# Self-attention's output projection of six token tiles as 2 by 2 blocks, with the sequences in another order

## The chip, the cores and the metric

The kernel runs on one core of a Trainium2 chip. The metric is the device time of one execution in microseconds; three runs of the kernel before gave 1006.05 us as the median, from 1003.74 to 1006.45. A profile of one execution tells when each engine was busy and what it waited for. The engines are TensorE (PE; its weight loads are shown apart as PEld), VectorE (DVE), ScalarE (ACT), GpSimd (POOL) and SyncE (SP), which here issues DMAs. Each engine works through its own queue in order, and waits on semaphores that others raise.

## The reference

One decoder layer in fp32: x + self-attention(norm(x)), then cross-attention to a context, then a mixture of experts with a shared expert. The change touches the first part alone. There are 8 sequences of 112 tokens, width 512, 16 heads of 128:

```
k, q, v = W_K x, W_Q x, W_V x        # per head: 128 x 512
attn = softmax(causal mask of q k / sqrt(128))
z = attn v                           # per head: 112 x 128
out = W_O z_flat                     # W_O: 512 x 2048 (16 heads x 128)
x = x + out
```

## The kernel before

The 896 tokens are kept as 7 tiles of 128. Tile t holds the 112 tokens of sequence t + 1 and 16 tokens of sequence 0, so sequence 0 is spread over the ends of all tiles (`seq` and `like_seq` translate). The layer norm's output is kept transposed in `xn1`.

Self-attention goes through four groups `g` of four heads (`GH`), and in each group through these steps.

- *Queries and keys* (`pair_of_heads`, matmuls on line 274): qT and kT, channels by tokens, for two heads at a time. These products are already done as 2 by 2 blocks: seven products of sums in place of eight products, with the sums of the tokens (`xc`) made once, and the sums of the weights made on GpSimd for each pair (`t`, pool `w_sums`, tag `wc`, three buffers).
- *Values* (`values_left`, `values`, line 393): the same scheme, seven products of 128 x 256 for each of three pairs of tiles. `values` is a generator; every `next` emits one product. Some rows are moved with DMAs from SP: each sequence's values must start at partition 0, and the 16-row tails of sequence 0 are gathered into `vals[0]`.
- *Each sequence b*: `softmax` (scores s on TensorE, line 191; scale, mask and maximum on VectorE; exponentials on ACT), `normalise` (reciprocal on VectorE, product on GpSimd, line 216), `turn` (transposes on TensorE, line 222, copy on ACT), `weighted` (z on TensorE, line 230, copy into `zT` on VectorE, line 237).
- *Output projection* (`project_o`, line 432): for tile t, four matmuls of 128 x 512, one for each head, added up in PSUM with `wog`, this group's part of W_O; VectorE adds the result to `xs[t]` (line 439). In the last group the statistics of the second norm are taken straight after it (`ln_stats`, into `mv2`).

The order in which these are written out is that of the loop at the end of the group: five sequences (1, 2, 3, 0, 4) go through softmax beside the value products; then one sequence after the other is weighted, with the softmax of the one that comes four later and the turning of the next one before it. Sequence 0 is weighted with sequence 4, and tiles are projected from there on, the last three at the end. A scheduler then orders the instructions of each engine by these priorities, and each engine keeps that order. The matmuls' results go through eight PSUM buffers: four in pool `mm` (q products, values, projection) and four in `sc` (k products, scores, turned scores, z). The first group's `wcp` buffers, `part` buffers (`p1`, `p5`, `u2`, `u3`, two each) and `qT`, `kT`, `zT` (one buffer each) are shared by all steps and groups.

After the last group, cross-attention starts with the key projections of the first context (three chunks, line 517), and with the second norm: standard deviations of tiles 0 to 3 in one instruction, of tiles 4 to 6 in another.

Of the kernel before, what the change touches and what calls it, by code (L numbers as in the profile page):

```python
# [15 lines left out]
F32 = mybir.dt.float32  # L16
I32 = mybir.dt.int32
AF = mybir.ActivationFunctionType
ALU = mybir.AluOpType
AX = mybir.AxisListType  # L20

P = 128
B, S, D = 8, 112, 512
NT = B * S
TT = NT // P
SP = P - S
ND = D // P
HALF = NT // 2
H, DH = 16, 128
GH = 4  # L30
NG = H // GH
# [28 lines left out]
def seq(ap, b):  # L60

    if b:
        return ap[..., (b - 1) * P : (b - 1) * P + S]
    axes = " ".join("abcd"[: len(ap.shape) - 1])
    return ap.rearrange(f"{axes} (t i) -> {axes} t i", t=TT)[..., S:]


def like_seq(ap, b):

    if b:  # L70
        return ap
    axes = " ".join("abcd"[: len(ap.shape) - 1])
    return ap.rearrange(f"{axes} (t i) -> {axes} t i", t=TT)
# [3 lines left out]
def decoder_layer(  # L77
    ctx: ExitStack, tc: tile.TileContext, x, ctxT, wqk, wv_all, wo, wx, wgate, wsgu, wsd, wegu, wed_a, wed_b, consts, out
):
    nc = tc.nc  # L80
# [7 lines left out]
    mm = ctx.enter_context(tc.tile_pool(name="mm", bufs=4, space=PSUM))  # L88
# [14 lines left out]
    xs = []  # L103
# [13 lines left out]
    def psum(pool, name):  # L117
        return pool.tile([P, 512], F32, tag=pool.name, name=name)
# [18 lines left out]
    def ln_begin(name):  # L137
        return lnpool.tile([P, TT, 2], F32, tag="mv", name=f"mv_{name}")

    def ln_stats(mv, t):  # L140
        st = lnpool.tile([P, 6], F32, tag="st", name="st")
        nc.vector.bn_stats(st, xs[t])
        nc.vector.bn_aggr(mv[:, t, :], st)
# [32 lines left out]
    mv2 = ln_begin("2")  # L176
    with ExitStack() as sa:
        wvpool = sa.enter_context(tc.tile_pool(name="weights_vo", bufs=2))
        xcp = sa.enter_context(tc.tile_pool(name="x_sums", bufs=1))
        wcp = sa.enter_context(tc.tile_pool(name="w_sums", bufs=3))  # L180
        up = sa.enter_context(tc.tile_pool(name="part", bufs=2))
# [6 lines left out]
        def softmax(b, qT, kT, q0):  # L188
            ps = psum(sc, "s")
            for h in range(GH):  # L190
                nc.tensor.matmul(  # L191
                    like_seq(ps[:S, h * S : (h + 1) * S], b),
                    qT[:, h, (b - 1) * P : (b - 1) * P + S] if b else q0[:, h, :],
                    seq(kT[:, h, :], b),
                    start=True,
                    stop=True,
                )
            s = sp.tile([S, GH, S], F32, tag="s", name="s", bufs=5)
            nc.vector.scalar_tensor_tensor(
                out=s,  # L200
                in0=ps[:S, : GH * S].rearrange("q (h p) -> q h p", h=GH),
                scalar=float(DH) ** -0.5,
                in1=mask[:, None, :].to_broadcast([S, GH, S]),
                op0=ALU.mult,
                op1=ALU.add,
            )
            mx = sp.tile([S, GH], F32, tag="mx", name="mx")
            nc.vector.tensor_reduce(mx, s, AX.X, ALU.max, negate=True)  # L208
            sm = sp.tile([S, GH], F32, tag="sm", name="sm")
            for h in range(GH):  # L210
                nc.scalar.activation(s[:, h, :], s[:, h, :], AF.Exp, bias=mx[:, h : h + 1], accum_out=sm[:, h : h + 1])  # L211
            return s, sm

        def normalise(s, sm):
            nc.vector.reciprocal(sm, sm)  # L215
            nc.gpsimd.tensor_tensor(s, s, sm[:, :, None].to_broadcast([S, GH, S]), ALU.mult)  # L216
            return s

        def turn(s):
            pt = psum(sc, "pT")  # L220
            for h in range(GH):
                nc.tensor.transpose(pt[:S, h * S : (h + 1) * S], s[:, h, :], ident[:S, :S])
            sT = sp.tile([S, GH, S], F32, tag="sT", name="sT")
            nc.scalar.copy(sT, pt[:S, : GH * S].rearrange("p (h q) -> p h q", h=GH))
            return sT

        def weighted(b, sT, v, zT):
            pz = psum(sc, "z")
            for h in range(GH):
                nc.tensor.matmul(  # L230
                    pz[:, h * S : (h + 1) * S],
                    v[:S, h * DH : (h + 1) * DH],
                    sT[:, h, :],
                    start=True,
                    stop=True,
                )
            nc.vector.tensor_copy(
                seq(zT, b), like_seq(pz[:, : GH * S].rearrange("p (h q) -> p h q", h=GH), b)
            )
# [58 lines left out]
        for g in range(NG):  # L298
# [11 lines left out]
            wog = wvpool.tile([P, 4, 512], F32, tag="w", name=f"wo_{g}")  # L310
# [9 lines left out]
            qT = qkp.tile([P, GH, NT], F32, tag="qT", name="qT")  # L320
            kT = qkp.tile([P, GH, NT], F32, tag="kT", name="kT")
            zT = zp.tile([P, GH, NT], F32, tag="zT", name="zT")
            for h in range(0, GH, 2):
                for w, dst, pool in ((wq, qT, mm), (wk, kT, sc)):
                    if g == 0 and h == 0 and dst is qT:

                        for half in range(2):
                            cols = bass.ds(half * HALF, HALF)
                            for i in range(2):
                                ps = psum(mm, "qk")  # L330
                                for c in range(ND):
# [4 lines left out]
                                        start=(c == 0),  # L336
                                        stop=(c == ND - 1),
# [10 lines left out]
            soft, turned, vals = {}, {}, {}  # L348
# [20 lines left out]
            wide = D // 2  # L369
# [59 lines left out]
            def project_o(t):  # L429
                ps = psum(mm, "o")  # L430
                for h in range(GH):
                    nc.tensor.matmul(  # L432
                        ps,
                        zT[:, h, t * P : (t + 1) * P],
                        wog[:, h, :],
                        start=(h == 0),
                        stop=(h == GH - 1),
                    )
                nc.vector.tensor_tensor(xs[t], ps, xs[t], ALU.add)  # L439
                if g == NG - 1:  # L440
                    ln_stats(mv2, t)


            q0 = vp.tile([P, GH, S], F32, tag="q0", name="q0", bufs=1)
            nc.gpsimd.tensor_copy(like_seq(q0, 0), seq(qT, 0))
            values_left()
            products = values()
            for b in (1, 2, 3, 0, 4):
                weights = softmax(b, qT, kT, q0)
                next(products)  # L450
                next(products)
                soft[b] = normalise(*weights)
                next(products)
            turned[1] = turn(soft.pop(1))
            for b in range(1, B):
                for _ in zip(range(3), products):
                    pass
                if b + 4 < B:
                    weights = softmax(b + 4, qT, kT, q0)
                if b + 1 < B:  # L460
                    turned[b + 1] = turn(soft.pop(b + 1))
                if b == 3:
                    turned[0] = turn(soft.pop(0))
                weighted(b, turned.pop(b), vals.pop(b), zT)
                if b == 4:
                    weighted(0, turned.pop(0), vals.pop(0), zT)
                if b + 4 < B:
                    soft[b + 4] = normalise(*weights)
                if b > 3:
                    project_o(b - 4)  # L470
            for t in range(B - 4, TT - 2):
                project_o(t)
            project_o(TT - 2)
            project_o(TT - 1)

# [5 lines left out]
    with ExitStack() as xa:  # L483
# [13 lines left out]
        rawk, rawq, keys, queries, turned = {}, {}, {}, {}, {}  # L497
# [75 lines left out]
        def product(x, w):  # L573
            ps = psum(mm, "kv")
            for c in range(2):
                nc.tensor.matmul(ps[:MC, :], x[:, c, :], w[:, c, :], start=(c == 0), stop=(c == 1))  # L576
            return ps[:MC, :]
# [191 lines left out]
        for b in range(B):  # L769
# [29 lines left out]
            if b + 1 < B:  # L799
# [9 lines left out]
                if b + 2 == B:  # L809
                    sw = [load_shared(i) for i in range(2)]  # L810
                    ahead = wpool.tile([P, 4, 512], F32, tag="w", name="ahead")
# [10 lines left out]
    with ExitStack() as ff:  # L822
# [37 lines left out]
        part = rp.tile([P, NT], F32, name="part")  # L860
# [275 lines left out]
        for i in range(2):  # L1136
            g = gp.tile([P, HALF], F32, tag="g", name="g")
# [20 lines left out]
        h = {}  # L1158
# [109 lines left out]
```

## Time and profile before

| What | us |
|---|---|
| Median of three runs | 1006.05 |
| Profiled execution | 1006.36 |
| Its span, first to last instruction | 1004.6 |
| TensorE busy | 983.2 |
| VectorE, ACT, GpSimd busy | 388.0, 304.5, 284.2 |
| Start of the value products (line 364) of groups 0 to 3 | 61.9, 166.3, 270.8, 375.3 |
| Start of the key projections of cross-attention (line 517) | 437.7 |
| Granted clock of TensorE, mean | 0.999 |

A group of heads takes 104.5 us from one of these starts to the next. In a line of the groups, the names are out<-in, the shapes partitions x elements, then the number of instructions, the busy time in us, the mean of one in ns, and the idle time just before them. An fp32 matmul shows as two records on PE, each with its weight load on PEld; the records overlap, so that the pace is the distance from one start to the next and not the length of a record.

### The profile page before, as it was taken

Reading aid. Unit: us, or ns where it says so; the run is one execution under the profiler, and the core shown is the slowest. Engines: PE = TensorE matmul, PEld = TensorE weight load, DVE = VectorE, ACT = ScalarE, POOL = GpSimd, SP = SyncE. Lnnn points to the kernel's source line nnn. Section 1 sums busy time; section 2 is a strip of 40 time slices with the busy share of each in tenths; the row PEclk is TensorE's granted clock in tenths of the full one; section 3 lists DMA queues with packets and bytes.
Section 4 is the critical chain, followed back from the end, with each engine's and each line's share of the span. In section 5 each row is a group of like instructions: output and inputs, shape, how many; then the busy total and the mean of one; then the engine's idle time right before and its main releaser. Section 6 shows DMA issues by size and latency. Waiting matters only on the chain.

```text
span 1004.6 us, 15494 instructions
## 1 busy us (share of the span) xinstructions
PE 983.2 (98%) x5876; PEld 555.8 (55%) x5876; DVE 388.0 (39%) x765; ACT 304.5 (30%) x750; POOL 284.2 (28%) x310
## 2 busy tenths in 40 slices
PE   5999999999999999999999999999999999999998
PEld 3468555954596458645455555555565544444433
DVE  3335223622263235445432443434325243333324
ACT  2135011500152005314354455546543111111100
POOL 4245034603450243122533322331205600000032
PEclk9999999999999999999999999999999999999999
DMA  9522012201211112000000010000209748777765
GB/s 347 199 92 76 4 38 85 65 19 42 84 36 49 42 45 67 14 1 0 31 33 5 29 32 32 29 4 1 86 19 423 258 120 257 237 237 234 218 191 157
DMA packets 35320, 98.85 MB, mean 98 GB/s; under 512 B 4848, under 2 KB 10224, under 8 KB 31664
## 3 DMA queue, kind: packets, MB, share of 16 engines
q1 hardware_dynamic: 30192, 85.26, 25.6%
q0 software_dynamic: 2320, 7.63, 2.3%
q10 hardware_dynamic: 2736, 4.98, 1.7%
q8 instruction: 47, 0.77, 0.3%
q14 instruction: 25, 0.20, 0.1%
HBM read 78.85 MB, written 14.94 MB: 93 GB/s over the span
## 4 chain that ended last, share of the span: by engine, by line
PE 92%; issue 3%; DVE 2%; POOL 1%; DMA 1%; ACT 1%; SPq 0%; DVEq 0%; POOLq 0%; ACTq 0%
PE qk L274 16%; PE o L432 10%; PE kv L576 9%; PE v L393 7%; PE gu L838 5%; PE xs L671 5%; PE gate L1074 5%; PE y L1096 4%; PE up L1074 4%; PE pv L696 4%; PE ys L1122 3%; PE k L517 3%; PE xv L517 3%; PE z L230 3%; PE s L191 3%
## 5 line engine op out<-in xcount | busy, mean ns | idle before, releaser
L679 ACT ACTIVATE e<-xs 125x448 f32<-125x448 f32 x192 | 88.4, 544 | 72.4 <-PE xs L671 72.4
L432 PE MATMUL o<-wo,zT 128*128 128x512 f32 x224 | 99.3, 595 | 0.0
L274 PE MATMUL qk<-xc,wc 128*128 128x448 f32 x180 | 70.1, 539 | 0.0
L432 PEld LDWEIGHTS o<-wo,zT 128*128 128x128 f32 x224 | 41.3, 190 | 46.2 <-issue 45.9
L1107 POOL DMA_INDIRECT got<-routed,at x14 | 15.1, 1080 | 172.2 <-issue 171.2
L1074 PE MATMUL gate<-wex,xT 128*64 x144 | 55.3, 466 | 0.5 <-ACT xT L1039 0.5
L838 PE MATMUL gu<-xn,sw 128*128 128x448 f32 x144 | 55.5, 541 | 0.0
L211 ACT ACTIVATE s<-s,mx 112x112 f32<-112x112 f32 x128 | 48.1, 377 | 23.5 <-DVE mx L208 14.9
L1074 PE MATMUL up<-wex,xT 128*64 x144 | 54.3, 459 | 0.0
L274 PEld LDWEIGHTS qk<-xc,wc 128*128 128x128 f32 x180 | 34.2, 190 | 33.5 <-issue 32.3
L671 PE MATMUL xs<-qT,kT 32*125 32x224 f32 x768 | 50.4, 373 | 1.5 <-DVE qT L634 1.5
L671 PEld LDWEIGHTS xs<-qT,kT 32*125 32x125 f32 x768 | 33.2, 181 | 32.5 <-issue 27.7
L1024 DVE COPY xn<-wex 128x704 f32 x60 | 31.2, 524 | 51.5 <-PE up L1074 51.5
L274 PE MATMUL qk<-xn,w 128*128 128x448 f32 x120 | 50.2, 539 | 0.0
L1096 PE MATMUL y<-wd,hT 128*64 128x512 f32 (+1 forms) x216 | 49.5, 592 | 0.6 <-ACT y L1100 0.6
L284 ACT COPY p<-qk 128x448 f32<-128x448 f32 x15 | 8.0, 532 | 137.0 <-PE qk L274 137.0
L439 DVE TENSOR_TENSOR x<-o,x 128x512 f32<-128x512 f32 x28 | 19.4, 691 | 75.8 <-PE o L432 75.8
L216 POOL TENSOR_TENSOR s<-s,sm 112x448 f32<-112x448 f32 x32 | 29.9, 934 | 61.5 <-DVE sm L215 55.6
L1074 PE MATMUL gate<-xn,xT 128*64 128x352 f32 x120 | 45.9, 464 | 0.0
L1074 PE MATMUL up<-xn,xT 128*64 128x352 f32 x120 | 45.3, 459 | 0.0
L291 POOL TENSOR_TENSOR qT<-p,u 128x448 f32<-128x448 f32 x7 | 7.9, 1132 | 122.8 <-DVE u L290 122.8
L506 POOL TENSOR_TENSOR sq<-kraw 125x512 f32<-125x512 f32 x24 | 25.2, 1049 | 59.4 <-ACT kraw L540 37.3
(232 smaller groups left out, 1846.5 us busy)
## 6 DMA issues: line engine op xcount, KB each, us to landing
wd<-in_wed_a SPq DMA_DIRECT2D x27, 512.0 KB, 4.4
wex<-in_wegu SPq DMA_DIRECT2D x8, 1408.0 KB, 19.3
wd<-in_wed_b SPq DMA_DIRECT2D x36, 192.0 KB, 4.7
w<-in_wqk SPq DMA_DIRECT2D x6, 1024.0 KB, 5.1
ctx<-in_ctxT SPq DMA_DIRECT2D x8, 750.0 KB, 4.2
slots<-zeros SPq DMA_DIRECT2D x1, 4608.0 KB, 19.7
wd<-in_wed_a SPq DMA_DIRECT2D x18, 256.0 KB, 4.4
routed<-y SPq DMA_DIRECT2D x18, 256.0 KB, 3.3
```

Source lines behind the costliest of these rows:

```text
L211: nc.scalar.activation(s[:, h, :], s[:, h, :], AF.Exp, bias=mx[:, h : h + 1], accum_out=sm[:, h : h + 1])
L274: nc.tensor.matmul(ps[:, :HALF], wt[:, c * P : (c + 1) * P], x[:, c, :], start=(c == 0), stop=(c == 1))
L393: nc.tensor.matmul(ps[:, :wide], x[:, c, cols], w[:, c, :], start=(c == 0), stop=(c == 1))
L432: nc.tensor.matmul(ps, zT[:, h, t * P : (t + 1) * P], wog[:, h, :], start=(h == 0), stop=(h == GH - 1),)
L517: nc.tensor.matmul(ps[:MC, :], ctxs[b][:, c, m * MC : (m + 1) * MC], w[:, c, :], start=(c == 0), stop=(c == ND - 1),)
L576: nc.tensor.matmul(ps[:MC, :], x[:, c, :], w[:, c, :], start=(c == 0), stop=(c == 1))
L671: nc.tensor.matmul(strips[j][:MC, ci * 2 * S : (ci + 1) * 2 * S], keys[b][rows, 2 * cp + ci, m * MC : (m + 1) * MC], queries[b][rows, 2 * ...
L679: last_exp[(b, cp, m)] = nc.scalar.activation(e[:, :, j, :, :].rearrange("p c e s -> p c (e s)"), strips[j][:MC, : 4 * S].rearrange("p (c ...
L696: nc.tensor.matmul(ps[VW * j : VW * (j + 1), g * S : (g + 1) * S], v[:, m, 16 * cp + h, :], es[m][:, h // 8, (h % 8) // 2, h % 2, :], star ...
L838: nc.tensor.matmul(ps[:, :HALF], w[:, c, i % 2, k, :], xn3[:, c, cols], start=(c == 0), stop=(c == ND - 1))
L1074: nc.tensor.matmul(gu[k][n, :FF], xT[:, c, n], w, start=(c == 0), stop=(c == ND - 1))
L1096: nc.tensor.matmul(ps[n, :], hT[:fn, i, n], w[i][:fn], start=(i == 0), stop=(i == len(FCH) - 1))
```

## The change

Six of the seven tiles are projected in pairs (0,4), (1,5), (2,6), for all four heads of the group, as one product of 2 by 2 blocks: the rows of blocks are the two tiles, the inner blocks two heads each, the columns of blocks the halves of the output's 512 columns. Seven products of two matmuls of 128 x 256 take the place of eight such blocks (sixteen such matmuls). Tile 3 keeps `project_o`.

For this, the sums of `wog` are made once in each group (`output_sums`, four subtractions of 128 x 512 on GpSimd, in two `wc` buffers), and the sums of the two tiles' zT for each pair (four of 128 x 256 on GpSimd, kept in kT, whose scores have all been issued by then). One product is copied from PSUM by ACT, and the others are added up by VectorE in the `part` buffers; the four blocks of results are added to `xs` by GpSimd, in the last group by VectorE, which then takes the statistics of both tiles.

The sequences go in the order 1, 5, 0, 2, 6, 3, 7, 4: five of them run ahead beside the value products, of which four are now emitted for each sequence (so that all are emitted before the first sequence is weighted), and the softmax of a later one follows five places behind. A pair is projected after sequences 0, 6 and 7.

```diff
+            def output_sums():
+                for i in range(2):
+                    w = wcp.tile([P, 4, wide], F32, tag="wc", name=f"wos{i}")
+                    wos.extend((w[:, 0:2, :], w[:, 2:4, :]))
+                nc.gpsimd.tensor_tensor(wos[0], o12, o11, ALU.subtract)
+                nc.gpsimd.tensor_tensor(wos[1], o22, wos[0], ALU.subtract)
+                nc.gpsimd.tensor_tensor(wos[2], o22, o12, ALU.subtract)
+                nc.gpsimd.tensor_tensor(wos[3], o21, wos[1], ALU.subtract)
+
+            def project_pair(lo, hi):
+                z = [zT[:, :, t * P : (t + 1) * P] for t in (lo, hi)]
+                (a11, a12), (a21, a22) = ((t[:, 0:2, :], t[:, 2:4, :]) for t in z)
+                room = kT.rearrange("p h n -> p (h n)")[:, lo * 4 * wide : (lo + 1) * 4 * wide]
+                s1, s2, s3, s4 = (
+                    room[:, k * wide : (k + 1) * wide].rearrange("p (h n) -> p h n", h=2) for k in range(4)
+                )
+                nc.gpsimd.tensor_tensor(s1, a21, a22, ALU.add)
+                nc.gpsimd.tensor_tensor(s2, s1, a11, ALU.subtract)
+                nc.gpsimd.tensor_tensor(s3, a11, a21, ALU.subtract)
+                nc.gpsimd.tensor_tensor(s4, a12, s2, ALU.subtract)
+
+                def product(x, w):
+                    ps = psum(mm, "o")
+                    for h in range(2):
+                        nc.tensor.matmul(ps[:, :wide], x[:, h, :], w[:, h, :], start=(h == 0), stop=(h == 1))
+                    return ps[:, :wide]
...
+                add = nc.vector.tensor_tensor if g == NG - 1 else nc.gpsimd.tensor_tensor
+
+                def onto(t, cols, a):
+                    add(xs[t][:, cols], xs[t][:, cols], a, ALU.add)
+
+                left, right = slice(0, wide), slice(wide, D)
+                p1, u, u3, w = part("p1"), part("u2"), part("u3"), part("p5")
+                nc.scalar.copy(p1, product(a11, o11))
+                p6 = product(s2, wos[1])
+                nc.vector.tensor_tensor(u, p6, p1, ALU.add)
+                nc.vector.tensor_tensor(p1, product(a12, o21), p1, ALU.add)
+                onto(lo, left, p1)
+                nc.vector.tensor_tensor(u3, product(s3, wos[2]), u, ALU.add)
+                p5 = product(s1, wos[0])
+                nc.vector.tensor_tensor(w, p5, u3, ALU.add)
+                nc.vector.tensor_tensor(u, p5, u, ALU.add)
+                onto(hi, right, w)
+                nc.vector.tensor_tensor(u3, product(a22, wos[3]), u3, ALU.add)
+                onto(hi, left, u3)
+                nc.vector.tensor_tensor(u, product(s4, o22), u, ALU.add)
+                onto(lo, right, u)
+                if g == NG - 1:
+                    ln_stats(mv2, lo)
+                    ln_stats(mv2, hi)
...
-            for b in (1, 2, 3, 0, 4):
+            order = (1, 5, 0, 2, 6, 3, 7, 4)
+            ahead = 5
+            for b in order[:ahead]:
                 weights = softmax(b, qT, kT, q0)
                 next(products)
                 next(products)
                 soft[b] = normalise(*weights)
                 next(products)
+                next(products)
             turned[1] = turn(soft.pop(1))
-            for b in range(1, B):
-                for _ in zip(range(3), products):
-                    pass
-                if b + 4 < B:
-                    weights = softmax(b + 4, qT, kT, q0)
-                if b + 1 < B:
-                    turned[b + 1] = turn(soft.pop(b + 1))
-                if b == 3:
-                    turned[0] = turn(soft.pop(0))
+            for _ in products:
+                pass
+            for i, b in enumerate(order):
+                new = order[i + ahead] if i + ahead < B else None
+                if new is not None:
+                    weights = softmax(new, qT, kT, q0)
+                if i + 1 < B:
+                    turned[order[i + 1]] = turn(soft.pop(order[i + 1]))
                 weighted(b, turned.pop(b), vals.pop(b), zT)
-                if b == 4:
-                    weighted(0, turned.pop(0), vals.pop(0), zT)
-                if b + 4 < B:
-                    soft[b + 4] = normalise(*weights)
-                if b > 3:
-                    project_o(b - 4)
-            for t in range(B - 4, TT - 2):
-                project_o(t)
-            project_o(TT - 2)
-            project_o(TT - 1)
+                if new is not None:
+                    soft[new] = normalise(*weights)
+                if i == 0:
+                    output_sums()
+                if b in (0, 6, 7):
+                    t = max(b - 5, 0)
+                    project_pair(t, t + 4)
+            project_o(3)
```

In the lines left out above, `o11` to `o22` are the four blocks of `wog`, `wide` is 256, and `part` takes a buffer from the pool that the q and k products use.

## The prediction

> **What bounds the kernel now.** I read the page first, its busy times and its costliest groups.
>
> ```profile
> PE 983.2 (98%) x5876; PEld 555.8 (55%) x5876; DVE 388.0 (39%) x765; ACT 304.5 (30%) x750; POOL 284.2 (28%) x310
> ...
> L432 PE MATMUL o<-wo,zT 128*128 128x512 f32 x224 | 99.3, 595 | 0.0
> ```
>
> TensorE is busy for 98% of the span; the projection (line 432) is 99.3 us of it and is never preceded by idle time. Next the chain of work that ended last, over the first group of heads (start, length, what):
>
> ```profile
> 82.80 2.61 PE v L393 x12
> ...
> 97.14 0.45 PE z L230 x4
> 97.58 3.59 PE o L432 x8
> ...
> 106.33 3.45 PE o L432 x8
> 109.78 0.88 PE z L230 x8
> 110.66 13.75 PE o L432 x32
> ```
>
> It never leaves TensorE: in this stage every microsecond of matmuls, and every new gap between them, is a microsecond of the total. It also gives the two prices that I need. 32 records of 512 columns take 13.75 us, 0.430 each; 12 records of 256 columns (the value products, which have the shape of the new ones) take 2.61 us, 0.217 each. So half the width costs half the time, and the additional weight loads stay hidden. An fp32 matmul has two records.
>
> Last, the timelines of VectorE, TensorE and GpSimd around the first projection, for what a hand-over costs (start, length, engine, line, operation, idle time before it):
>
> ```profile
> 96.44 0.17 DVE L215 RECIPROCAL sm<-sm 112x4 f32<-112x4 f32 x1
> 96.79 0.62 DVE L237 COPY zT<-z 128x448 f32<-128x448 f32 x1 [0.19 <-PE z L230]
> ```
> ```profile
> 94.80 1.95 PE L230 MATMUL z<-sT,v 112*128 112x112 f32 x16
> ...
> 97.47 3.70 PE L432 MATMUL o<-wo,zT 128*128 128x512 f32 x8
> ```
> ```profile
> 85.31 0.72 POOL L268 TENSOR_TENSOR wc<-w 128x256 f32<-128x256 f32 x1
> 85.99 0.73 POOL L267 TENSOR_TENSOR wc<-w,wc 128x256 f32<-128x256 f32 x1
> 86.80 0.73 POOL L269 TENSOR_TENSOR wc<-w,wc 128x256 f32<-128x256 f32 x1
> ...
> 96.75 0.94 POOL L216 TENSOR_TENSOR s<-s,sm 112x448 f32<-112x448 f32 x1 [1.42 <-PE z L230]
> ```
>
> The z matmuls end at 96.75 and the copy starts at 96.79: 0.04. The reciprocal ends at 96.61 and GpSimd's product starts at 96.75: 0.14; other such waits are nearer 0.1, and I take 0.12. The copy ends at 97.41 and TensorE starts at 97.47: 0.06, and this first piece of eight records takes 3.70 against 3.61 elsewhere: resuming costs 0.1 more. GpSimd issues additions of 128x256 every 0.68 us and each lasts 0.73.
>
> **The change, part by part.**
>
> *Fewer matmul columns.* For a pair of tiles, before: 2 x 4 matmuls of 512 columns, 16 records x 0.430 = 6.88 us. After: 7 products x 2 matmuls of 256, 28 records x 0.217 = 6.08. That is 0.80 less, 12 pairs in four groups: 9.6 us less. It lies wholly on the chain.
>
> *The token sums, a new wait.* Product 1 of a pair needs no sum, but product 2 multiplies s2, and GpSimd makes s1, s3, s2, s4 in that order as built, after the pair's last sequence has been copied into zT. From the end of the last z record: 0.04, the copy 0.62, 0.12, three sums 0.68 + 0.68 + 0.73 = 2.09, 0.06; together 2.93. Meanwhile TensorE has what the built order puts between that z and product 2, less 0.16, by which the z record's end lies behind the start of the next one.
> - Pair (0,4), after sequence 0: turning sequence 6 (0.39), three of the four z matmuls of sequence 2 (0.67), product 1 (0.87): 1.93 - 0.16 = 1.77. Wait 1.16; but the normalisation of sequence 7 (0.93 on GpSimd) stands just before these sums and ends some 0.4 too late, so 1.6.
> - Pair (1,5), after sequence 6: product 1 (0.87), turning 7 (0.39), half of sequence 3's z (0.45): 1.55. Wait 1.4.
> - Pair (2,6), after sequence 7: product 1 and z of sequence 4 (0.89): 1.60. Wait 1.3 to 1.4; I take 1.35.
>
> The sum is 4.35, with three resumptions 4.65 a group, 18.6 in all. In the last group VectorE, not GpSimd, adds the results to x and takes the statistics; an addition (0.42) and a statistic or two (0.69 each) stand before the copy of sequence 7, some 1.0 us more, once: 19.6. Queued behind the waiting product 2 are the other five products and the z and turn matmuls that feed the next pair, so nothing fills the gap.
>
> *The wait that goes.* The first projection of each group waited 0.05 for zT and resumed at 0.1: 0.15 x 4 = 0.6 less. Product 1 of the new order has zT in time by 0.1 to 0.3.
>
> *Weight sums.* Four subtractions of 128x512 on GpSimd, 1.27 each (the row of the value weights' sums, line 377): 5.1 a group. They stand among the normalisations, while TensorE has value products; GpSimd is busy 13.1 of 20 us there (window 180 to 200). Nothing on the chain; if that cover went, each would delay one normalisation by at most 1.27. They also hold two of three buffers of the operand sums of the next q and k products; only one pair of heads can be prepared ahead, and the next pair's sums (4 x 0.73) fit in the 10.5 us of its matmuls.
>
> *Results.* Per pair seven VectorE additions of 0.42 and an ACT copy of 0.36 instead of two of 0.69: 3.0 us under 6.1 us of products. GpSimd adds to x, 4 x 0.75 a pair, in groups 0 to 2, behind which no sum of the next pair is late: its zT copy is later still. In the last group the four additions are VectorE's, 1.7 more. Zero, except for the 1.0 above.
>
> *Sequences reordered.* Same instructions. Sequence 0 is now weighted third and needs the 16-row tails, four to seven DMAs of 0.46 to 0.60 on SP each with 1.8 to 1.9 to landing; by the rows the last lands some 0.9 us before its use. Zero, at worst 1.2 in each group if a landing takes its longest, 3.1. Tile 3 is projected last, so the norm of tiles 0 to 3 starts after it; the three key chunks (10.5 us of matmuls) cover the 7 us that it needs, as they do now for tiles 4 to 6. Zero.
>
> *A rule weighed.* The row is 0.73 us for a GpSimd addition of 128x256 against 0.42 on VectorE (line 401). The Trainium skill, "GPSIMD Engine Reference", section "Engine selection", says to put two-input elementwise work on VectorE, since GpSimd is about half as fast, and 1.96 is its measured ratio; that speaks against where these sums stand. By its ratio, as an estimate, a sum would last 0.83 and the total would be 3.7 us higher; by the row it stays as it is, and the row is taken.
>
> *Sum.* -9.6 + 19.6 - 0.6 = **+9.4 us**. The profiled execution took 1006.36 (span 1004.6 and 1.8 around it), so 1015.8; it lies 0.3 above the median of 1006.05, against which I predict **1015.5 us**.
>
> **Bounds.** A GpSimd sum is at least 0.63 (the 128x250 sums of line 571, fastest) and three of them save 0.3 a pair, 3.6 in all; the hand-over to GpSimd may be 0.05, 0.8 less: 1011. Upwards, 0.3 more a pair, a second late copy behind VectorE in the last group and a late landing give 1020. Range 1010.5 to 1020.5.
>
> **The rivals.**
> *The sums are hidden (faster).* If product 2 waited less than 0.80 a pair the change would gain; with no wait at all, 1006.05 - 9.6 - 0.6 = 996. It decides where the way from z to s2 takes 2.2 instead of 2.93, that is, where a sum takes 0.48. For it: GpSimd is busy only 28%. Against: no row of this shape lies below 0.63, and 28% is an average; the sums can't start before the copy. 5%.
>
> *TensorE falls to half pace after each gap (much slower).* At the start the same matmuls ran at half pace:
>
> ```profile
> 14.27 8.68 PE L332 MATMUL qk<-xn,w 128*128 128x448 f32 x16 [0.68 <-ACT xn L161]
> ```
>
> 16 records of 448 columns are 6.0 us elsewhere (112 of them in 42.09 us on the chain, 0.376 each), so 2.7 are lost; after each of 12 gaps that would be 32 us: 1048. Against it, after an idle time of 1.47 us:
>
> ```profile
> 493.35 1.04 PE L671 MATMUL xs<-qT,kT 32*125 32x224 f32 x16 [1.47 <-DVE qT L634]
> 494.32 1.98 PE L576 MATMUL kv<-wx,ctx 128*125 128x512 f32 x4
> ```
>
> four records of 512 in 1.98, as later. 3%.
>
> *VectorE or the scratch in kT holds the products up too.* The next group's keys go where the sums stood, and seven products share four PSUM buffers. A second gap as long as the first in each pair would be 17 more: 1032. For it: the last group has 8 us of VectorE work in a pair. Against: a period of 10 us. 4%.
>
> **How the numbers follow.** The likeliest case, gaps of about 1.5 at product 2 of each pair, has 88%, of which 1 lies within 0.3% of before (1003.0 to 1009.1, about what a measurement can tell from no change). Slower: 87 + 3 + 4 = 94, of which I move 2 to "same" for hand-overs that I cannot see. The range leaves out both slow rivals, the fast one and some 5% of the main case.
>
> **What would show it.** Right: product 2 of every pair preceded by 1.2 to 1.8 us of TensorE idle time that GpSimd's kT ends; new matmuls 0.217 apart; a group of 106.5 us instead of 104.4; the stages after 450 us shifted, not changed. Wrong: no such idle time (the first rival), spacings of 0.43 after it (the second), or other products waiting for VectorE (the third).

## The result, and the profile after

| | median, us | runs | ratio to the kernel before, 95% interval |
|---|---|---|---|
| before, run beside it | 1005.16 | 1003.74 to 1006.45 | |
| changed kernel | 1011.94 | 1011.45 to 1015.20 | 1.0072 (1.0058 to 1.0085) |
| the same once more, on another occasion | 1014.65 | 1011.44 to 1015.11 | 1.0089 (1.0068 to 1.0110) |

Each ratio goes by the runs of the kernel before that were made beside it (in the second comparison their median was 1005.91). The change makes the kernel slower by 5.8 to 8.5 us in the first comparison and by 6.8 to 11.1 in the second; 1015.5 was forecast, 9.4 above before.

The two profiled spans differ by only 5.0 us (1009.6 against 1004.6). It helps to cut them by stage: from the first value products (line 364) to the first key projection of cross-attention, which is where all of the change lies, the kernel before takes 375.8 us and the changed one 384.1, **8.3 us more**. Before that stage the profiled execution of the changed kernel is 2.7 us shorter, and after it 0.5. The first of these is not the change's doing, as the last section shows; so the experiments below are read by this stage as well as by their times.

The page of the changed kernel, busy times and the group of the products that read the token sums, and then two lines of its list of waits (us in total, times, longest):

```profile
PE 973.2 (96%) x6020; PEld 582.1 (58%) x6020; DVE 410.2 (41%) x837; ACT 309.2 (31%) x762; POOL 364.3 (36%) x410
...
L473 PE MATMUL o<-wos,kT 128*128 128x256 f32 x144 | 36.2, 388 | 15.7 <-POOL kT L466 15.7
```
```profile
PEld o L473 <- POOL kT L466: 18.7, 12, 2.3
...
PE o L473 <- POOL kT L466: 15.7, 12, 2.1
```

TensorE has 10 us less to do and is idle for longer than that: 12 waits, one for each pair, all ended by line 466, which is s2 on GpSimd. The chain of work, which before never left TensorE in this stage, now leaves it at every pair (second group, start, length, what):

```profile
197.94 0.02 issue
...
198.07 0.46 POOL s L216
198.53 0.43 issue
198.96 0.73 POOL kT L465
199.69 0.68 POOL kT L467
200.37 0.69 POOL kT L466
201.06 0.04 issue
201.10 5.46 PE o L473 x24
...
217.19 0.91 PE z L230 x8
218.10 0.02 issue
218.12 0.64 DVE zT L237
218.76 0.07 issue
218.82 0.73 POOL kT L465
219.55 0.68 POOL kT L467
220.24 0.69 POOL kT L466
220.93 0.04 issue
220.97 5.45 PE o L473 x24
226.42 3.43 PE o L432 x8
```

The third pair (from 217.19) is the forecast path, step for step: z, copy, hand-over, s1, s3, s2, hand-over, product 2. In the first pair the sums stand behind the last normalisation (line 216), as was forecast too. A group of heads takes 106.3 us from one start of its value products to the next, 104.5 before.

### The profile page after: what moved, and what is told of

Same layout as the page of the kernel before. It is cut to its first block, busy times and chain, and to the rows that moved or that the text cites. A ratio compares the mean times of both kernels' runs of the same rounds, so it can differ in the third digit from the quotient of the medians.

```text
span 1009.6 us, 16049 instructions
## 1 busy us (share of the span) xinstructions
PE 973.2 (96%) x6020; PEld 582.1 (58%) x6020; DVE 410.2 (41%) x837; ACT 309.2 (31%) x762; POOL 364.3 (36%) x410
## 4 chain that ended last, share of the span: by engine, by line
PE 86%; POOL 4%; issue 4%; DVE 3%; DMA 1%; ACT 1%; SPq 0%; DVEq 0%; POOLq 0%; ACTq 0%
PE qk L274 16%; PE kv L638 9%; PE v L393 7%; PE o L473 6%; PE gu L900 5%; PE xs L733 5%; PE gate L1136 5%; PE y L1158 4%; PE up L1136 4%; PE pv L758 4%; PE ys L1184 3%; PE xv L579 3%; PE k L579 3%; PE s L191 2%; PE o L432 1%
## 5 line engine op out<-in xcount | busy, mean ns | idle before, releaser
L473 PE MATMUL o<-wos,kT 128*128 128x256 f32 x144 | 36.2, 388 | 15.7 <-POOL kT L466 15.7
L900 PEld LDWEIGHTS gu<-xn,sw 128*128 128x128 f32 x144 | 26.8, 190 | 24.2 <-issue 24.2
L638 PE MATMUL kv<-wx,ctx 128*125 128x512 f32 x84 | 40.4, 603 | 0.0
L758 PE MATMUL pv<-e,v 125*32 125x112 f32 x1536 | 40.1, 260 | 0.0
```

Source lines behind the costliest of these rows:

```text
L473: nc.tensor.matmul(ps[:, :wide], x[:, h, :], w[:, h, :], start=(h == 0), stop=(h == 1))
L758: nc.tensor.matmul(ps[VW * j : VW * (j + 1), g * S : (g + 1) * S], v[:, m, 16 * cp + h, :], es[m][:, h // 8, (h % 8) // 2, h % 2, :], star ...
L900: nc.tensor.matmul(ps[:, :HALF], w[:, c, i % 2, k, :], xn3[:, c, cols], start=(c == 0), stop=(c == ND - 1))
```

## The experiments

In the table, the stage is the one from the first value products to the first key projection, in each run's own profile; the gaps are the time by which product 2 starts later than the pace of TensorE would have it, for the pairs (0,4), (1,5), (2,6) of the second group, and for (2,6) of the last group; the 0.1 us that each resumption costs comes on top. The column on the group is the time from the second start of the value products to the third. The ratios of e1 to e8 go by other runs of the kernel before, made beside each (medians 1005.91 to 1006.03); e2 and e3 have ten runs, e8 two, the others four.

| | median, us | ratio, 95% interval | group, us | stage, us | gaps, us | last group's (2,6) |
|---|---|---|---|---|---|---|
| before | 1005.16 | | 104.5 | 375.8 | | |
| changed | 1011.94 | 1.0072 (1.0058 to 1.0085) | 106.3 | 384.1 | 1.53, 1.34, 1.30 | 2.25 |
| e1, sums on VectorE | 998.22 | 0.9922 (0.9897 to 0.9947) | 102.4 | 368.8 | 0.23, 0.07, 0 | 1.56 |
| e2, free products first | 1002.30 | 0.9967 (0.9954 to 0.9980) | 102.9 | 371.7 | 0, 0.34, 0.45 | 0.64 |
| e3, order alone | 1004.95 | 0.9996 (0.9984 to 1.0007) | 104.4 | 376.7 | none | tile 3: 1.32 |
| e4, sums unread | 994.67 | 0.9891 (0.9868 to 0.9914) | 101.8 | 365.5 | none | none |
| e5, one sum twice | 1022.18 | 1.0169 (1.0150 to 1.0188) | 109.2 | 393.7 | 2.12, 1.92, 1.32 | 2.39 |
| e6, statistics after tile 3 | 1010.97 | 1.0060 (1.0042 to 1.0078) | 106.3 | 383.1 | 1.53, 1.34, 1.30 | 1.29 |
| e7, VectorE sums and order | 995.22 | 0.9894 (0.9878 to 0.9911) | 102.2 | 366.9 | none | 0.29 |
| e8, one sum three times | 1039.79 | 1.0332 (1.0302 to 1.0363) | 112.8 | 410.8 | 2.71, 2.39, 2.12 | 3.93 |

The theory under test is that of the prediction: the change saves matmul columns and pays for them with the gap before product 2, whose length is that of the way through the copy and three GpSimd sums. The rivals were that the new order of the sequences, or the narrower matmuls, or the work added to other engines, cost the time.

### e1: the token sums on VectorE

```diff
-                nc.gpsimd.tensor_tensor(s1, a21, a22, ALU.add)
-                nc.gpsimd.tensor_tensor(s2, s1, a11, ALU.subtract)
-                nc.gpsimd.tensor_tensor(s3, a11, a21, ALU.subtract)
-                nc.gpsimd.tensor_tensor(s4, a12, s2, ALU.subtract)
+                nc.vector.tensor_tensor(s1, a21, a22, ALU.add)
+                nc.vector.tensor_tensor(s2, s1, a11, ALU.subtract)
+                nc.vector.tensor_tensor(s3, a11, a21, ALU.subtract)
+                nc.vector.tensor_tensor(s4, a12, s2, ALU.subtract)
```

> The four token sums of each pair on VectorE instead of GpSimd, nothing else. Theory (the time is that of the gap before product 2, which the GpSimd sums set): three sums take 0.34 + 0.34 + 0.42 = 1.1 us instead of 2.09 and need no hand-over from the copy, so each gap of 1.3 to 1.5 us falls to 0.0 to 0.4, and the time to 996 to 1000 us, below the kernel before (1005.2). Rival (the new order of the sequences, or the narrow matmuls, cost the time): it stays at 1010 to 1013.

998.22 us: the same change, with 48 instructions on another engine, is faster than the kernel before. The timeline of VectorE shows, for pair (0,4) of the second group, the path that took 2.8 us on GpSimd:

```profile
195.87 0.62 DVE L237 COPY zT<-z 128x448 f32<-128x448 f32 x1
196.53 0.78 DVE L465 TENSOR_TENSOR kT<-zT 128x256 f32<-128x256 f32 x1
197.24 0.41 DVE L467 TENSOR_TENSOR kT<-zT 128x256 f32<-128x256 f32 x1
197.57 0.41 DVE L466 TENSOR_TENSOR kT<-kT,zT 128x256 f32<-128x256 f32 x1
```

From the start of the copy to the end of s2 are 2.11 us; in the changed kernel, from 218.12 to 220.93 on the chain above (pair (2,6)), 2.81. The first sum lasts 0.78 in this pair and 0.42 to 0.43 in the other two, where the path takes 1.76 (copies at 204.80 and 213.58, s2 ready at 206.56 and 215.34). In the first three groups the gaps are nearly gone. In the last group, where VectorE also adds the results to x and takes the statistics, one gap of 1.56 is left.

### e2: the products that need no token sum first

```diff
-                p6 = product(s2, wos[1])
+                p7 = product(a12, o21)
+                p3 = product(a22, wos[3])
+                p6 = product(s2, wos[1])
                 nc.vector.tensor_tensor(u, p6, p1, ALU.add)
-                nc.vector.tensor_tensor(p1, product(a12, o21), p1, ALU.add)
+                nc.vector.tensor_tensor(p1, p7, p1, ALU.add)
...
-                nc.vector.tensor_tensor(u3, product(a22, wos[3]), u3, ALU.add)
+                nc.vector.tensor_tensor(u3, p3, u3, ALU.add)
```

> Sums stay on GpSimd; the two other products that need no token sum (a12 o21 and a22 with its weight sum) are written out between product 1 and the one that needs s2. Theory: up to 1.74 us more work stands before the wait, so the gaps fall to 0.0 to 0.5, somewhat more in the last group: 998 to 1002 us. Rival (order or narrow matmuls): 1010 to 1013.

1002.30, 0.3 above what was expected. The sums take as long as in the changed kernel, but TensorE has more to do meanwhile: this moves the same wait from the other side. It gains less than e1, since two gaps of 0.3 and 0.4 remain in each group, and in the last one 0.93, 0.64, and 1.47 before tile 3. Part of its time has nothing to do with the sums: behind the stage its profile takes 569.6 us where all others take 566 to 567, for a stretch of 6.8 us at half clock in cross-attention (last section). Seven of its ten runs have a mean granted clock of 0.996; the three at 0.999 took 1000.85 to 1001.18.

### e3: the order alone

```diff
-                if i == 0:
-                    output_sums()
                 if b in (0, 6, 7):
                     t = max(b - 5, 0)
-                    project_pair(t, t + 4)
+                    project_o(t)
+                    project_o(t + 4)
```

> The new order of the sequences with the old projection of 512 columns at the same three places, no sums. Theory: the order costs nothing, 1003.5 to 1007 us, no gap over 0.2 us before a projection except one in the last group, where tile 3 comes last. Rival (the order costs the time): 1010 to 1013.

No difference from before (0.9984 to 1.0007). The order has one price, once, in the last group: TensorE is idle for 1.15 us before tile 3, until a copy of z, since it is now projected straight after the last sequence (e3, TensorE):

```profile
432.94 3.70 PE L432 MATMUL o<-wo,zT 128*128 128x512 f32 x8 [1.15 <-DVE zT L237]
```

### e4: the sums made but not read

```diff
+                unread = {id(s1): a11, id(s2): a12, id(s3): a21, id(s4): a22}
+
                 def product(x, w):
+                    x = unread.get(id(x), x)
```

> As the changed kernel, with all sums made, but the products that should read token sums read blocks of zT instead: the sums of the tokens are left out of the result. Theory: no gap is left and only the 9.6 us of fewer columns and the 0.6 us of the old wait remain: 993 to 997 us. Rival (the narrow matmuls, or GpSimd's and VectorE's additional work, cost the time): above 1003.

994.67: all instructions of the changed kernel are there, and the dependence on the token sums alone is missing. Its chain in the second group stays on TensorE again:

```profile
195.32 0.67 PE z L230 x6
195.99 6.06 PE o L476 x28
202.05 0.21 PE z L230 x2
202.26 0.38 PE pT L222 x4
202.64 0.89 PE z L230 x8
203.53 6.06 PE o L476 x28
```

28 records in 6.06 us are 0.216 each, as forecast. The stage is 10.3 us shorter than before, and 18.6 shorter than in the changed kernel: these are the gain and the loss, measured apart.

### e5 and e8: one token sum made twice, and three times

```diff
                 nc.gpsimd.tensor_tensor(s1, a21, a22, ALU.add)
+                nc.gpsimd.tensor_tensor(s1, a21, a22, ALU.add)
```

(e8 has the line a third time.)

> The changed kernel with the first token sum of each pair made twice on GpSimd (the same instruction again, 0.68 us). Theory (these sums stand on the path from zT to product 2): pairs (0,4) and (1,5) wait 0.6 to 0.7 us longer; before pair (2,6) the scheduler has put one more product, so its wait stays near 1.4: 107.5 us a group instead of 106.3, 1015 to 1019 us in all. Rival (the sums are hidden, another hand-over sets the gap): gaps and time as the changed kernel's, 1010 to 1013.

The gaps of (0,4) and (1,5) grew by 0.6, that of (2,6) did not, as expected; but 1022.18 lies above what was expected: the first group took 107.5 us, as expected, the second and the third 109.2. The gaps together are 4.6 us longer than in the changed kernel, the stage 9.7. The rest is TensorE's clock (e5, columns: the window and its length, busy time of PE, PEld, DVE, ACT and POOL with the number of instructions, the granted clock, and the DMAs' share and GB/s):

```profile
92.00:96.00 4.00, 2.12 (x16) 1.83 (x14) 1.44 (x5) 2.33 (x11) 3.68 (x5) 1.00 0.24 100
96.00:100.00 4.00, 3.93 (x18) 3.49 (x19) 1.45 (x4) 0.00 (x0) 2.35 (x4) 1.00 0.00 0
199.50:203.50 4.00, 2.12 (x16) 1.84 (x14) 1.44 (x5) 2.33 (x11) 3.68 (x5) 1.00 0.21 90
203.50:207.80 4.30, 4.22 (x12) 3.44 (x13) 0.85 (x2) 0.00 (x0) 2.13 (x4) 0.60 0.00 0
```

After the gap of the first group the clock stays at 1.00; after the same gap of the second, 12 matmul records fit into a window of 4.3 us, where 4.0 hold 18 in the first. The third and the fourth group go like the second. Each slow stretch is 3.4 us at a clock of 0.5, and loses 1.7: three of them 5.1, and 4.6 + 5.1 = 9.7.

> The first token sum of each pair made three times on GpSimd, for longer gaps: 2.2 to 2.8 us before product 2, one of 4 in the last group. If a gap of about 2 us is what lowers TensorE's clock, the profile shows the granted clock at 0.5 for 3.4 us after most of the twelve gaps, 1.7 us lost each time: by the gaps alone 1025 to 1029 us, with the clock 1035 to 1048. If the three stretches of the run with the sum made twice were chance, a few at most and 1025 to 1033.

1039.79, which is what was expected with the clock and not without it. Eight stretches of 3.4 us at 0.5 stand in its profile and lose 13.6 us, and its gaps are 13.1 longer than those of the changed kernel: together 26.7, and the stage is 26.7 longer.

### e6: the statistics after tile 3

```diff
-                if g == NG - 1:
-                    ln_stats(mv2, lo)
-                    ln_stats(mv2, hi)
...
             project_o(3)
+            if g == NG - 1:
+                for t in (0, 4, 1, 5, 2, 6):
+                    ln_stats(mv2, t)
```

> The changed kernel with the statistics of all six paired tiles taken after tile 3's projection in the last group; nothing else. Theory: the longer gap of 2.25 us before pair (2,6) of the last group comes from the two statistics that stand before the copy of sequence 7 on VectorE, and falls to 1.3 as in the other groups; 1 us less than the changed kernel in all (1010 to 1013), which the timing may not resolve, but the profile will. Rival (VectorE's additions to x make it): the gap stays over 1.8.

The gap fell from 2.25 to 1.29 and the stage by 1.0. In the changed kernel, VectorE has two statistics ahead of the copy of sequence 7 (starts at 431.72):

```profile
429.99 0.41 DVE L483 TENSOR_TENSOR x<-x,u 128x256 f32<-128x256 f32 x1
430.43 1.29 DVE L142 BATCH_NORM_STATS2 st<-x 128x6 f32<-128x512 f32 x2
431.64 0.16 DVE L143 BATCH_NORM_AGGREGATE mv<-st 128x2 f32<-128x6 f32 x1
431.72 0.59 DVE L237 COPY zT<-z 128x448 f32<-128x448 f32 x1
```

In e6 the copy follows the addition at 430.90. The times of the two kernels alone (1010.97 and 1011.94) wouldn't have told it.

### e7: both remedies

e1 with `p7 = product(a12, o21)` ahead of the product that needs s2, and in the last group:

```diff
-                add = nc.vector.tensor_tensor if g == NG - 1 else nc.gpsimd.tensor_tensor
+                add = nc.vector.tensor_tensor if g == NG - 1 and lo == 2 else nc.gpsimd.tensor_tensor
...
-                if g == NG - 1:
-                    ln_stats(mv2, lo)
-                    ln_stats(mv2, hi)
...
+            if g == NG - 1:
+                for t in (0, 4, 1, 5):
+                    ln_stats(mv2, t)
             project_o(3)
+            if g == NG - 1:
+                for t in (2, 6):
+                    ln_stats(mv2, t)
```

> A version meant to beat both: token sums on VectorE, the product a12 o21 before the one that needs s2, in the last group GpSimd adds the results of the first two pairs, and the statistics stand around tile 3. Theory: gaps of 0.0 to 0.2 before product 2 in the first three groups and of at most 0.5 in the last, 102.2 us a group, 996 to 999 us in all. Rival (VectorE, now with the sums and the additions, holds the products up): 1000 or more.

995.22 us, 0.9894 (0.9878 to 0.9911), 0.8 below what was expected: 8.9 us under the kernel before by the stage (366.9), 1.4 above e4, which waits for no token sum. This is the version to keep.

### e9: the changed kernel again

> The changed kernel itself, for another profile. Its eleven gaps of 1.3 to 1.5 us leave the granted clock at 1.0 as in the first profile; the one of 2.25 us in the last group may now be followed by 3.4 us at 0.5. 1010 to 1015 us.

The gaps are the same to 0.02 us and no stretch at a lower clock stands in this profile either, not even after the gap of 2.25. This profile is of the fastest of the four runs, 1011.44; the other three took 3.1 to 3.7 us longer, and where they lost them is not on record.

## Why the prediction was right, and where it was off

- *Fewer columns*: right. -9.6 for the columns and -0.6 for the wait that goes were forecast; e4 shows -10.3 for both.
- *The gaps*: right in place, cause and size. 1.6, 1.4 and 1.35 were forecast, 1.53, 1.34 and 1.30 are there. e1 (faster sums), e2 (more work before the wait), e4 (no dependence) and e5 (slower sums) each moved the gap in the way that the path says, and e4 alone takes all of it away.
- *The last group*: 1.0 more was forecast, from an addition and the statistics; 0.95 is there, and e6 shows that the statistics make it.
- *Sequences reordered, at zero*: right in the changed kernel, by e3 within 0.2% of the total. The 1.3 and 1.5 us that tile 3 costs in e3 and e2 had not been named; in the changed kernel they don't arise, since product 2 and its followers stand between the last copy and tile 3.
- *The sum*: 9.4 was forecast and the stage shows 8.3 (the medians lie 6.8 and 8.7 above before; they take in the start of the kernel, which varies by 2.4). The term that was too large is that of the gaps, 19.6 against 18.6 (changed kernel less e4): the gaps add up to 17.6 where 18.4 was forecast, 0.06 less at each of twelve, and what is left for the twelve resumptions is 1.0, 0.08 each instead of 0.1.
- *The rule that was weighed*: the forecast took the row of 0.73 us for a GpSimd sum, and it is 0.73 in the changed kernel (line 465, 728 ns). The advice of the Trainium skill, "GPSIMD Engine Reference", section "Engine selection", to put such work on VectorE, is borne out by e1: 0.41 to 0.42 for lines 466 to 468 there, and with it the sign of the whole change turns.
- *The first rival, hidden sums*: out, by the twelve waits. Its point of decision (a way of 2.2 us from z to s2) was not tested as such; e1 agrees with it, where the way takes 1.8 to 2.2 and the change gains.
- *The second rival, half pace after each gap*: didn't happen in either profile of the changed kernel. Two of its eight runs (1015.20 and 1015.11 us) have a mean granted clock of 0.997, so that slow stretches did occur there, and their place is not on record. The price of 2.7 us a gap, taken from the start of the kernel, was too high: a slow stretch loses 1.7. And the row that was held against it (1.47 us of idle time, full pace afterwards) could not exclude it: e5 and e8 show the mechanism after gaps half a microsecond longer, and the last section shows it once, elsewhere, after a shorter one, and what sets the cases apart.
- *The third, VectorE or the scratch in kT*: out. No other product waits in the changed kernel, and with the sums added to VectorE (e7) the time is the lowest of all kernels that compute the whole result.

## What to carry to other kernels

Where one engine carries the whole chain, an algorithm that saves its work is worth the saving less the latency of what it now depends on: count the way from the last producer to the first consumer, each hand-over included, and set against it what the bound engine has to do meanwhile. Work on an engine with much idle time is not free when it stands on such a way; choose the engine there by latency, and put the products that need nothing new first. A gap of 2 us can cost 1.7 more than its length, when TensorE's clock falls after it. Measure gain and loss apart by a kernel that makes the new operands and doesn't read them: it tells at once how much there is to win back.

## What the runs showed of the hardware

- *TensorE falls to half clock for 3.4 us after some idle gaps of 2 to 4 us.* By idle time before product 2 (the gap of the table less 0.15 us): none of fifty gaps of 0.2 to 1.8 us was followed by it. At 1.96 us it was three of seven (e5, e8), at 2.09 none of two (changed kernel, twice), at 2.23 four of five, at 2.57 three of four, and at 3.8 the only one. So between 2 and 2.6 us it is not the length alone that decides.

- *Where the gap falls decides with it.* In each profile, all changes of the granted clock are whole multiples of 3.413 us apart: in e5 the slow stretches start at 204.21, 313.44 and 422.67, which is 32 such steps each time, and in e8 at 208.30 and 221.96, four steps. If a run is cut into these steps, the same gap of 1.96 us of e5 lies across a border in the first group (94.98) and within one step in the second (first fence, columns as above): TensorE is busy for 2.54 and 2.33 us of the two steps there, and for 1.45 of the one here, and only this one is followed by half clock. In the stage, over all eleven profiles, the eleven steps that were followed by half clock are those in which TensorE was busy for 21 to 43%, and in all others it was busy for 45% or more.

- *The limit is not the same everywhere.* In cross-attention of e2's profile a step with 53% was followed (second fence), while steps with 57% were not (e2 and before), and the last steps of a kernel, up to 58%, were. That step of e2 holds two idle times, 0.53 and 1.07 us; in e1 the same two are spread over two steps (third fence), and the matmuls after them took 1.09 us where e2's took 1.81 (fourth and fifth fence, TensorE's timeline in e2 and in e1). No run moves a gap against the steps, so this is a reading of the traces that no experiment has tested, and why the slow state of e2 lasted two steps is open. The Trainium skill, "TensorE: Matmul & The Clock Gate", section "Part 1: The HAM clock gate (the "warmup" mystery)", puts the return to half clock behind an idle window of about 3.4 us that runs freely; the steps of 3.413 us agree with it, but steps with 1.6 to 2.7 us of idle time were enough here, and the measurement decides.

```profile
91.57:94.98 3.41, 2.54 (x20) 2.26 (x18) 1.87 (x5) 2.76 (x12) 2.74 (x4) 1.00 0.40 166
94.98:98.40 3.42, 2.33 (x11) 2.07 (x12) 0.72 (x2) 0.00 (x0) 2.57 (x4) 1.00 0.00 0
200.80:204.21 3.41, 1.45 (x8) 1.16 (x7) 0.80 (x2) 1.08 (x5) 3.25 (x5) 1.00 0.00 0
204.21:207.62 3.41, 3.41 (x10) 2.70 (x9) 0.85 (x2) 0.00 (x0) 1.31 (x3) 0.50 0.00 0
```
```profile
678.60:682.01 3.41, 1.81 (x15) 1.29 (x14) 3.14 (x6) 2.17 (x5) 0.67 (x1) 1.00 0.00 0
682.01:685.43 3.42, 3.42 (x14) 2.54 (x13) 1.09 (x2) 1.17 (x2) 0.00 (x0) 0.50 0.00 0
685.43:688.84 3.41, 3.41 (x36) 2.48 (x37) 0.00 (x0) 2.21 (x5) 0.00 (x0) 0.50 0.00 0
```
```profile
676.65:680.07 3.42, 2.48 (x15) 1.43 (x13) 3.42 (x7) 2.86 (x7) 0.67 (x1) 1.00 0.00 0
680.07:683.48 3.41, 2.75 (x22) 2.14 (x26) 1.60 (x4) 1.74 (x4) 0.00 (x0) 1.00 0.00 0
```
```profile
681.79 1.81 PE L160 MATMUL ln_t<-cst,xn 128*128 128x128 f32 x8 [1.07 <-DVE v L663]
```
```profile
680.73 1.09 PE L160 MATMUL ln_t<-cst,xn 128*128 128x128 f32 x8 [1.07 <-DVE v L661]
```

- *The start of the kernel varies by 2.4 us from one execution to the next.* The first 16 records of line 332 run partly at half pace: 8.68 us in the profile of before, 6.28 in that of the changed kernel, 8.15 in e1, 7.91 in e4, 6.28 in e2 and e3. The trace's record of the granted clock begins, at 1.0, at 19.13 us in the profile of before and at 12.88 in that of the changed kernel (a window ahead of that is printed as 1.00 all the same). In before, a start of these matmuls at 14.27 with half pace up to 19.13 loses 2.43, and over all eleven profiles this working gives their time to 0.04 us. So the loss depends on where the first matmuls fall between the steps of the clock. This is most of the 2.7 us by which the stages before the change differ, and explains why spans of single profiles (5.0 us apart) understate what the change costs (8.3).

```profile
13.93 6.28 PE L332 MATMUL qk<-xn,w 128*128 128x448 f32 x16 [0.68 <-ACT xn L161]
```
